# A two-layer graph network: the loads of the natural layouts and the first left operands get other places in the order of work

## The chip, the cores and the metric

The kernel runs on one core of one Trainium2 chip, in float32. The metric is the device time of one execution in microseconds (us): before the change 1774.37, the median of three runs (1773.52 to 1776.88).

## The reference, cut to what matters

`x` has 16 batches of 1024 nodes with 128 features; `adj` is a dense 1024 x 1024 matrix. Layer 0 is one graph convolution, layer 1 five steps of a gated graph unit; both are applied to a normalised, rectified input and added to `x`.

```python
# layer 0
h = relu(layernorm(x));  x = x + adj @ (h @ weight) + bias
# layer 1
h = relu(layernorm(x))
for _ in range(5):
    m  = adj @ h                          # in_matrix = out_matrix = adj
    av = concat([m, m])
    u3 = h @ u3_w.T + u3_b
    z  = sigmoid(av @ w3_w.T + w3_b + u3)
    r  = sigmoid(av @ w4_w.T + w4_b + u3)
    hv = tanh(av @ w5_w.T + w5_b + (r * h) @ u5_w.T + u5_b)
    h  = (1 - z) * h + z * hv
x = x + h
```

## The kernel before, in words

**Tiling.** Four batches form a quad, and there are four quads. A step of layer 1 for one quad is an aggregation (`adj @ h` for the four batches, `aggregate`, L439) and then its gates (`gates`, L799), which run twice: with key "A" for batches 0 and 1 and with key "B" for batches 2 and 3. Two quads are worked on in turn, a step of the one and then a step of the other (L1233), so that the state which a step has updated is needed again only a step later. In the 20 steps stand two more aggregations, for layer 0 (`BLOCKS`, L75), and two plain ones run ahead of the steps.

**The aggregation.** It is a fast matrix multiplication in two levels with seven products each, so 49 small products. One small product is two fp32 matmuls of 128 x 128 with 128 x 256 (L504), each issued as two instructions. Its left operand is a sum of blocks of `h`, its right operand a sum of blocks of `adj`. The right operands are made once at the start and kept in DRAM; 9 of them are resident in SBUF, and the other 40 are streamed in pairs (512 KB) through `ring`, which holds six pairs. `stream` (L297) loads the pair that comes six pairs later into the room of the pair that has just been used. Pair 17 is thus loaded at place 29, pair 18 at place 31, pair 19 at place 33 and pair 0 of the next aggregation at place 36. The five loads after these are put among the gates (`GATE_LOADS`, L68). Pair 18 is first used by the product of place 45.

**Left operands.** `nat[:, k]` holds the state of batch k in the natural layout, with the nodes along the partitions. The left operands are made of it: blocks of `big` by ACT copies (L401) and by sums of DVE, and blocks of `little` (L424 to L427) by sums over `big`, by DVE. The first of them for the next aggregation are made ahead, among the gates: `early_pieces` (L432) returns 12 pieces in the order

1. two ACT copies from nat[0] and nat[1],
2. four sums of `little`,
3. two more ACT copies from nat[0] and nat[1],
4. two sums of `big` from nat[2] and nat[3],
5. two more sums of `little`.

**Natural layouts.** The gates work on the transposed state. After the update, DVE transposes 32 x 32 squares (`squares_to_dram`, L664), SP stores them to a scratch in DRAM (fn<-sq), and `natural_from` (L673) loads them back as the natural layout with four DMAs of 128 KB for each batch (nat<-fn).

**What sets the order.** All is written out by hand. Every DMA is issued by SP, in program order, and a DMA that has to wait (for PE to have read a room of the ring, or for a store's data) holds up those behind it. Pieces of side work are put under a key by `put` (L708) and emitted when the program gets there by `place` (L711). Key k, 1 to 49, is after the k-th small product of the aggregation; "Ar0" to "Ar3" are after the r part of gates A for each of four halves of two batches, "Az0" to "Az3" after their z part, and the same with B. After z comes the third part (pv, tanh, hv), which has no keys.

Other side work at such keys: in some steps statistics for a later normalisation (`NORMS`, at r3, z1 and z3 of both gates, L788 to L790); in the aggregation after these the factors `nmr` (place 10), the ACT activations that use them, and the stores h<-ha or ft<-hb (places 22 and 36); in three steps transposed inputs (sqt<-ft, places 8, 18, 28 and 38); in eight steps the outputs of an earlier quad (loads at place 16, adds at 34, the store out_dram<-xt at 38).

**The lines touched.** `GATE_PLACES` (L975) has the places of the 12 early pieces, and the default of `loads_at` in `step` (L983) those of the four natural loads. `period(4)` is 30 and `period(5)` is 37. The very first step (L1231), and the loads for the aggregations of layer 0 (L1073), pass places of their own. The final step has no successor and loads nothing.

Of the kernel before, what the change touches and what calls it, by code (L numbers as in the profile page):

```python
# [96 lines left out]
def tile_two_gnn_layers(  # L97
# [30 lines left out]
    def dma(out, in_):  # L128
        pin(nc.sync.dma_start(out=out, in_=in_))
# [4 lines left out]
    def x_tile(b):  # L134
        return pre.tile([P, NC, D], F32, tag="xt", name=f"xt_{b}")

    def load_x(b, xt=None, parts=((0, NC),)):
        xt = xt if xt is not None else x_tile(b)
        for cs in parts:
            cs = slice(*cs)  # L140
            dma(xt[:, cs], by_slots(x[b])[:, cs])
        return xt
# [289 lines left out]
    def early_pieces(n):  # L432
        bigs, smalls = left_pieces(n)
        return bigs[0] + smalls[0] + bigs[1] + bigs[3] + smalls[1][:2]

    def period(i):
        return 2 + 7 * i
# [226 lines left out]
    def squares_to_dram(hT, nm):  # L664


        sq = flip_tile(f"sq_{nm}")
        for g in range(NH):
            pin(nc.vector.transpose(squares_of_half(sq, g), transposed_half(hT, g)))  # L669
        scratch, blocks = scratch_for("fn", nm)  # L670
        return lambda: dma(scratch, sq.rearrange("p k j e -> p (k j e)")), blocks
# [19 lines left out]
    def transposing(b, hT):  # L691

        box = {}

        def load():
            box["sq"] = flip_tile(f"sqt_{b}")
            dma(box["sq"].rearrange("p k j e -> p (k j e)"), parked[b][0])

        def turn():
            for g in range(NH):  # L700
                pin(nc.vector.transpose(transposed_half(hT, g), squares_of_half(box["sq"], g)))

        return load, turn
# [4 lines left out]
    def put(k, *pieces):  # L708
        fixed.setdefault(k, []).extend(pieces)
# [56 lines left out]
    def put_statistics(kind, first):  # L766

        rest = []
        for n, b in enumerate((first, first + 1)):
            box = {}  # L770

            def begin(b=b, box=box):
                box["n"] = Norm(xts[b], None, f"{kind}{b}")
                box["n"].statistics(range(CH))

            def relu(k, b=b, box=box):
                def run():
                    if k == 0:
                        box["n"].dst = flip_tile(f"h{kind}_{b}")
                    box["n"].relu(range(2 * k, 2 * k + 2))  # L780

                return run

            def done(b=b, box=box):
                (keep if kind == "a" else layer_1_input)(b, box["n"].dst)

            key = "AB"[n]
            put(f"{key}r3", begin)  # L788
            put(f"{key}z1", lambda box=box: box["n"].statistics(range(CH, NC)))
            put(f"{key}z3", lambda box=box: box["n"].scales(EVERY))  # L790
            rest.append((10, lambda box=box: box["n"].shift(EVERY)))
            rest += [(11 + 13 * n + 3 * k, relu(k)) for k in range(CH)]
            rest.append((22 + 14 * n, done))
            if kind == "a":
                rest.append((("Ar0", "Br0")[n], lambda b=b: bias(b)))
        return rest
# [175 lines left out]

    state = {}

    GATE_PLACES = ("Ar1", "Ar2", "Ar3", "Ar3", "Az0", "Az1", "Br1", "Br2", "Bz0", "Bz1", "Bz1", "Bz2")  # L975
    BLOCK_PLACES = (44, 46, 47, 47, 48, 48)

    def loads_of_next(source, places):

        for k, at in enumerate(places):  # L980
            put(at, lambda k=k: natural_from(source[k], nat[:, k]))

    def step(i, loads_at=(period(4), period(5), "Ar0", "Ar2"), early_places=GATE_PLACES):  # L983
        st = state[i]
        quad, n = st["quad"], st["step"]
        nm = f"{quad}_{n}"
        hT = [hT_all[:, i, k] for k in range(Q)]
        last = n == STEPS - 1
        final = last and quad == quads - 1
        other = state[1 - i]  # L990
        me = (quad, n)
        for k, piece in relus.pop("next", ()):
            put(k, piece)
        for b, k in LOADS.get(me, ()):
            put(k, lambda b=b: xts.update({b: load_x(b)}))
        if me in TRANSPOSED:
            q = TRANSPOSED[me]
            for k in range(Q):
                load, turn_it = transposing(q * Q + k, hT_all[:, q % 2, k])
                put(8 + 10 * k, load)  # L1000
                put(17 + 10 * k, turn_it)
        if me in OUTPUTS:
            for k, piece in zip((16, 34, 38), outputs[OUTPUTS[me]]):
                put(k, piece)
        block = BLOCKS.get(me)

        source = h0_of(block) if block else other["blocks"]
        if final:
            st["x1"] = []

            def load_x1(k):
                x1 = x_tile(f"1_{quad * Q + k}")
                dma(x1, x1s[quad * Q + k])
                st["x1"].append(x1)

            for k, places in enumerate(((None, 10, 13), (12, 24, 27), (26, 39, 41), (37, "R10", "R11"))):
                for piece, at in zip(outputs[(quad - 1) * Q + k], places):
                    if at is not None:
                        put(at, piece)
            for k, at in enumerate(("R00", "R01", "Z01", "V10")):  # L1020
                put(at, lambda k=k: load_x1(k))
        if source is not None:
            loads_of_next(source, loads_at)
        aggregate(nm, place)
        if me in NORMS:
            relus["next"] = put_statistics(*NORMS[me])
        if source is not None:
            for k, piece in zip(early_places, early_pieces(made[0])):
                put(k, piece)
        stored, ready = {}, {}  # L1030

        def turn(first):
            def run(k):
                k += first
                stored[k] = Later(lambda n: ready[k][n])

                def squares():
                    store, ready[k] = squares_to_dram(hT[k], f"{nm}_{k}")
                    if k >= Q - 2:
                        put({Q - 2: 4, Q - 1: 9}[k], store)  # L1040
                    else:
                        store()

                if k == Q - 1:
                    put(3, squares)
                else:
                    squares()

            return run

        if last:
            outputs.update({quad * Q + k: output(quad * Q + k, Later(lambda n, k=k: ready[k][n])) for k in range(Q)})
            if quad == quads - 2:
                put("Bz1", outputs[quad * Q][0])
        if final:
            last_gates(quad, hT, st["x1"])
            st["quad"], st["blocks"] = None, None
            return
        for a, key in enumerate("AB"):
            pair = slice(2 * a, 2 * a + 2)  # L1060
            gates(
                [mT[:, 2 * a + k] for k in range(2)],
                hT[pair],
                f"{nm}{key}",
                key,
                turn(2 * a),
            )
        st["step"] += 1
        st["blocks"] = [stored[k] for k in range(Q)]
        if last:  # L1070
            begin(i, quad + 2)
        if block:
            loads_of_next(other["blocks"], (period(3) + 4, period(4) + 4, period(5) + 2, period(6)))  # L1073
            pieces = early_pieces(made[0] + 1)
            for k, piece in zip(BLOCK_PLACES, pieces):
                put(k, piece)
            aggregate(f"a{block}", place, gates_follow=False)
            for k in range(Q):
                for g in range(NH):
                    po(block * Q + k, g)  # L1080
                    if 2 * k + g in (1, 2, 6, 7):
                        pieces[{1: 6, 2: 7, 6: 8, 7: 9}[2 * k + g]]()
            for piece in pieces[10:]:
                piece()
# [4 lines left out]
    def begin(i, quad):  # L1089

        if quad >= quads:
            state[i] = {"quad": None, "blocks": None}
            return
        state[i] = {"quad": quad, "step": 0, "blocks": parked_of(quad)}
# [13 lines left out]
    def h0_of(quad):  # L1108
        return Later(lambda k: h0_blocks[quad * Q + k])
# [120 lines left out]
    early_places = ("Br0", "Br1", "Br2", "Br2", "Br3", "Br3", "Br2", "Br3", "Bz0", "Bz1", "Bz2", "Bz2")  # L1230
# [45 lines left out]
```

## Time and profile before

| What | us |
|---|---|
| median of three runs | 1774.37 |
| the profiled execution's own time | 1779.16 |
| its span, first to last instruction | 1777.4 |
| PE busy (99% of the span) | 1761.9 |
| DVE busy (77%) | 1372.8 |
| ACT busy (51%) | 903.7 |
| one fp32 instruction 128 x 256 of the aggregation, mean | 0.380 |
| one ACT copy from nat (L401), median | 0.609 |
| one DVE sum of `little`, mean | 0.42 |

The granted TensorE clock is 0.999 of full speed. Matmul instructions overlap, so starts are compared rather than durations: where nothing waits, small products start every 0.863 us. DMA, all issued by SP: 396.9 MB, 223 GB/s on average; the loads of the ring are 440 of 512 KB, the natural loads nat<-fn 256 of 128 KB, with a median of 6.3 and 6.6 us from issue to landing.

How to read the rows: in the timeline a row is start, duration, engine, line, operation, output<-inputs and a count, and in brackets at its end the idle time before it with what ended it. PE is TensorE's matmul, DVE VectorE, ACT ScalarE, SPq the DMA issues of SyncE. In the table by windows each engine has busy time and instructions, then come the granted clock, the share of the DMA engines and GB/s.

### The profile page before, as it was taken

The numbers are of one execution on the slowest core, as the hardware profiler recorded it, in microseconds if no ns is written. First come the engines' busy times: TensorE is split into PE (matmuls) and PEld (weight loads), VectorE is DVE, ScalarE is ACT, GpSimd is POOL, SyncE is SP. The second block draws the span as 40 slices with busy tenths as digits, with TensorE's granted clock in tenths as the row PEclk, the third lists the DMA queues.
The fourth block names the chain that finished last, engine by engine and source line by source line (L and its number), as shares of the span: only waits on it lengthen the run. The fifth ranks groups of instructions, "written<-read, shape, count | busy, mean of one in ns | idle before, by whom it ended". The sixth has DMA issues, their size and how long they took to land.

```text
span 1777.4 us, 21433 instructions
## 1 busy us (share of the span) xinstructions
PE 1761.9 (99%) x6438; PEld 1200.4 (68%) x6438; DVE 1372.8 (77%) x2806; ACT 903.7 (51%) x1974; POOL 59.3 (3%) x41
## 2 busy tenths in 40 slices
PE   9999999999999999999999999999999999999998
PEld 3557667588586675858857667585776857667584
DVE  6778988776879687877687968777687777867787
ACT  5246556544555555554455554545445454445544
POOL 3101000000000000000000000000000000000000
PEclk9999999999999999999999999999999999999999
DMA  7489786688395856749839578694866849476794
GB/s 257 158 310 308 235 250 215 176 253 252 123 310 181 267 198 192 241 133 282 263 132 312 185 222 255 168 292 157 250 205 198 253 131 307 153 234 219 195 291 171
DMA packets 169970, 396.88 MB, mean 223 GB/s; under 512 B 18560, under 2 KB 88064, under 8 KB 169856
## 3 DMA queue, kind: packets, MB, share of 16 engines
q1 hardware_dynamic: 169856, 395.52, 70.8%
q8 instruction: 52, 0.85, 0.2%
q14 instruction: 62, 0.51, 0.1%
HBM read 314.44 MB, written 81.00 MB: 222 GB/s over the span
## 4 chain that ended last, share of the span: by engine, by line
PE 89%; DMA 5%; DVE 4%; ACT 1%; POOL 1%; issue 0%; SPq 0%; DVEq 0%; POOLq 0%
PE a L504 25%; PE c L504 12%; PE b L504 6%; PE a_a L504 3%; DMA ring<-rd 3%; PE pr_3B L808 2%; PE pr_1B L808 2%; PE pr_0B L808 2%; PE pr_2B L808 2%; PE pr_2A L808 2%; PE pr_1A L808 2%; PE pr_0A L808 2%; PE pr_3A L808 2%; PE a_a L620 2%; PE pv_0B L808 2%; PE pv_3B L808 2%
## 5 line engine op out<-in xcount | busy, mean ns | idle before, releaser
L504 PE MATMUL a<-ring,big 128*128 128x256 f32 x1120 | 288.3, 380 | 4.4 <-DMA ring<-rd 3.7
L523 ACT COPY Z<-a 128x256 f32<-128x256 f32 x480 | 177.2, 371 | 198.9 <-PE a L504 198.6
L241 DVE TENSOR_TENSOR Z<-Z,taps 128x512 f32<-128x512 f32 (+1 forms) x264 | 144.5, 554 | 167.2 <-ACT taps L523 166.9
L504 PE MATMUL c<-ring,little 128*128 128x256 f32 x960 | 246.6, 379 | 1.2 <-DMA ring<-rd 1.1
L504 PEld LDWEIGHTS a<-ring,big 128*128 128x128 f32 x1120 | 211.7, 190 | 43.5 <-issue 10.5
L241 DVE TENSOR_TENSOR mT<-mT,Z 128x1024 f32<-128x1024 f32 x154 | 188.3, 1223 | 27.4 <-ACT Z L523 22.3
L504 PEld LDWEIGHTS c<-ring,little 128*128 128x128 f32 x960 | 182.0, 190 | 26.9 <-ACT Z L523 1.5
L523 ACT COPY taps<-c 128x256 f32<-128x256 f32 x280 | 103.6, 370 | 117.2 <-PE c L504 112.5
L504 PE MATMUL b<-ring,big 128*128 128x256 f32 x560 | 143.8, 379 | 1.0 <-DMA ring<-rd 1.0
L504 PE MATMUL a<-resident,little 128*128 128x256 f32 x560 | 143.8, 379 | 0.0
L504 PE MATMUL a<-ring,little 128*128 128x256 f32 x560 | 143.7, 379 | 0.0
L504 PEld LDWEIGHTS b<-ring,big 128*128 128x128 f32 x560 | 106.3, 190 | 15.8 <-DMA ring<-rd 1.4
L504 PEld LDWEIGHTS a<-resident,little 128*128 128x128 f32 x560 | 106.3, 190 | 14.7 <-ACT Z L523 0.3
L504 PEld LDWEIGHTS a<-ring,little 128*128 128x128 f32 x560 | 106.4, 190 | 14.5
L669 DVE STREAM_TRANSPOSE sq<-hT_all 128x512 f32<-128x512 f32 x152 | 98.6, 687 | 0.0
L523 ACT COPY taps<-b 128x256 f32<-128x256 f32 x140 | 52.0, 372 | 56.7 <-PE b L504 55.8
L401 ACT COPY big<-nat 128x512 f32<-128x512 f32 x132 | 80.6, 614 | 0.1
L238 DVE TENSOR_TENSOR little<-little,big 128x256 f32<-128x256 f32 x154 | 65.4, 425 | 6.7
L238 DVE TENSOR_TENSOR little<-big 128x256 f32<-128x256 f32 x154 | 64.3, 418 | 0.0
L238 DVE TENSOR_TENSOR little<-big,little 128x256 f32<-128x256 f32 x154 | 64.2, 417 | 0.0
L241 DVE TENSOR_TENSOR little<-big 128x256 f32<-128x256 f32 x154 | 64.0, 416 | 0.2
L523 ACT COPY mT<-a 128x256 f32<-128x256 f32 x80 | 29.8, 372 | 48.1 <-PE a L504 48.0
(282 smaller groups left out, 2912.6 us busy)
## 6 DMA issues: line engine op xcount, KB each, us to landing
ring<-rd SPq DMA_DIRECT2D x440, 512.0 KB, 6.3
fn<-sq SPq DMA_DIRECT2D x76, 512.0 KB, 3.7
nat<-fn SPq DMA_DIRECT2D x256, 128.0 KB, 6.6
x1d<-xt SPq DMA_DIRECT2D x16, 512.0 KB, 5.9
sqt<-ft SPq DMA_DIRECT2D x16, 512.0 KB, 6.8
xt<-x1d SPq DMA_DIRECT2D x16, 512.0 KB, 7.6
xt<-in_x_dram SPq DMA_DIRECT2D x15, 512.0 KB, 6.2
out_dram<-xt SPq DMA_DIRECT2D x14, 512.0 KB, 7.9
```

The source lines that it names most:

```text
L238: pin(nc.vector.tensor_sub(o, a, b))
L241: pin(nc.vector.tensor_add(o, a, b))
L401: return [lambda i=i: pin(nc.scalar.copy(made_of(k, i), part(a, b, i))) for i in range(2)]
L504: nc.tensor.matmul(bank, l, right[:, c, :], start=opens and c == 0, stop=c == SB - 1, skip_group_check=True,)
L523: pin(nc.scalar.copy(to, bank))
L620: nc.tensor.matmul(bank, left[:, c, :], right[c // SB][:, c % SB], start=p in (1, 2, 5) and c == 0, stop=c == CH - 1, skip_group_check=True,)
L669: pin(nc.vector.transpose(squares_of_half(sq, g), transposed_half(hT, g)))
L808: nc.tensor.matmul(bank, w_sb[:, w, :], moving, start=start, stop=stop, skip_group_check=True)
```

## The change

Two tuples change; no instruction is added or removed. `loads_at` becomes 48, "Ar0", "Ar1", "Ar3" instead of 30, 37, "Ar0", "Ar2". In `GATE_PLACES` the first two copies go from "Ar1", "Ar2" to "Az0", "Az1", and the four sums of `little` from "Ar3", "Ar3", "Az0", "Az1" to "Az2", "Az2", "Az3", "Br0". The other six pieces stay.

```diff
@@ -972,7 +972,7 @@
-    GATE_PLACES = ("Ar1", "Ar2", "Ar3", "Ar3", "Az0", "Az1", "Br1", "Br2", "Bz0", "Bz1", "Bz1", "Bz2")
+    GATE_PLACES = ("Az0", "Az1", "Az2", "Az2", "Az3", "Br0", "Br1", "Br2", "Bz0", "Bz1", "Bz1", "Bz2")
     BLOCK_PLACES = (44, 46, 47, 47, 48, 48)
@@ -980,7 +980,7 @@
-    def step(i, loads_at=(period(4), period(5), "Ar0", "Ar2"), early_places=GATE_PLACES):
+    def step(i, loads_at=(48, "Ar0", "Ar1", "Ar3"), early_places=GATE_PLACES):
         st = state[i]
```

The pieces run by these places, unchanged:

```python
    def early_pieces(n):
        bigs, smalls = left_pieces(n)
        return bigs[0] + smalls[0] + bigs[1] + bigs[3] + smalls[1][:2]
```

## The prediction

> **What bounds the kernel now.** I read the page's busy line first, then the waits of the matmul engine, and then looked at the places of the few waits in the timeline.
>
> ```profile
> PE 1761.9 (99%) x6438; PEld 1200.4 (68%) x6438; DVE 1372.8 (77%) x2806; ACT 903.7 (51%) x1974; POOL 59.3 (3%) x41
> ```
>
> TensorE is busy for 99% of the span: it is the bound, and an edit that removes none of its instructions can only win back its idle time. The waits of PE (total us, times, longest) say whose idle time that is:
>
> ```profile
> PE a L504 <- DMA ring<-rd: 3.7, 5, 2.0
> PE c L504 <- DMA ring<-rd: 1.1, 1, 1.1
> PE b L504 <- DMA ring<-rd: 1.0, 1, 1.0
> PE a L504 <- ACT Z L523: 0.7, 3, 0.3
> ```
>
> Seven waits for a streamed right operand, three for a PSUM bank that ACT empties. To price a wait I take the distance between the starts of neighbouring products in PE's timeline and subtract 0.863 us, the distance where nothing waits (so the product after a wait, which starts 0.07 slow, is counted too). After the special start, in order of time: 0.52 (at 294, ACT), 2.20 (601, ring), 0.60 (678, ring), 0.67 (958, ring), 0.47 (1010, ACT), 1.38 (1102, ring), 0.94 and 0.29 (1114 and 1117, ring), 1.29 and 0.45 (1727 and 1729, ring): 8.81 us. The steps without a wait repeat every 76.63 us.
>
> Four of these places, 601, 678, 958 and 1114, are the same product: place 45, the first to use pair 18 of the ring. What stands ahead of that load on SP's queue, at the largest:
>
> ```profile
> 588.69 0.38 SPq L129 DMA_DIRECT2D ring<-rd  x1
> 589.17 2.26 SPq L129 DMA_DIRECT2D nat<-fn  x4
> 591.53 3.50 SPq L129 DMA_DIRECT2D ring<-rd  x3
> ...
> 600.90 5.35 SPq L129 DMA_DIRECT2D nat<-fn  x8
> ```
>
> ```profile
> 597.99 1.03 PE L504 MATMUL a<-ring,little 128*128 128x256 f32 x4
> 600.98 1.10 PE L504 MATMUL a<-ring,big 128*128 128x256 f32 x4 [1.96 <-DMA ring<-rd]
> ```
>
> The four transfers of nat[0] (place 30) are issued for 2.26 us; pair 18 (place 31) follows at 591.53, lands 9.3 us later, and PE, which could have used it at 598.85, starts at 600.98. The transfer engines are the crowded resource just there (an aggregation, its gates, and the aggregation with the stalls at 1102 and 1114):
>
> ```profile
> 1383.34:1425.69 42.35, 42.35 (x198) 37.28 (x197) 32.57 (x59) 19.55 (x51) 0.00 (x0) 1.00 0.93 290
> 1425.69:1460.00 34.31, 34.31 (x82) 15.18 (x81) 24.95 (x42) 18.20 (x28) 0.00 (x0) 1.00 0.36 118
> 1076.63:1118.98 42.35, 40.47 (x185) 34.73 (x185) 33.24 (x61) 18.13 (x48) 0.00 (x0) 1.00 1.02 309
> ```
>
> The last columns are granted clock, DMA share and GB/s: 93 to 102% of the engines in an aggregation, 36% among the gates, at full clock.
>
> **The change, part by part.** *SP's queue.* SP issues in program order, so what matters is what nat[0] passes. It goes from place 30 to 48: past pairs 18, 19 and 0 (places 31, 33, 36), and past the h/ft stores (place 36), sqt loads and out stores (place 38) where a step has them. nat[1] passes only what stands at place 38; nat[2] and nat[3] pass nothing, although their places are renamed. It happens in 18 steps; the first step, the final one and the two plain aggregations have places of their own. Per step 4 DMAs (512 KB) leave the crowded stretch, 512 KB / 290 GB/s = 1.8 us of all engines. Pair 18 can be issued as soon as the product of place 31 has ended: 2.4 us sooner in the steps at 601 and 958, 3.5 at 1114, but only 0.6 at 678, where PE itself is what it waits for; in each it also lands with 1.8 us less ahead of it. Against stalls of 2.20, 0.67, 1.23 and 0.60 that suffices: minus 4.70 us. The stalls at 1102 (pair 13, issued before nat[0]) and in the final step stay.
>
> A rule of the Trainium skill speaks against this move: "DMA: Bandwidth & Descriptors", section "Rules for kernel authors", says to overlap a transfer with compute by issuing it early and waiting late. By that rule postponing nat[0] can only lose, and the sum would be 0 or above. The row decides:
>
> ```profile
> DMA to landing us min/median/max: 2.1/6.4/11.6
> ```
>
> nat[0] and nat[1] now follow pair 0, roughly where nat[1] and nat[2] are issued today, and need that landing time. At 601 that is 600.90 to 606.25; today's last load of that group lands about 4.5 us after issue, at 611. The second copy would be due at about 613 (its place in the next paragraph, in a step without the stall). Early issue buys nothing beyond that, so I take the row; if the landing took 11.6, the rule would be right (the slower rival).
>
> *ACT.* The two copies of 0.61 us (L401) go from behind r1 and r2 to behind z0 and z1. In the step from 1425.69 the z activations run from 1433.46, 0.69 each, one per 0.86 of PE. With the copies between them: copy0 from 1434.15, z1 1434.8, copy1 1435.4, z2 1436.0, z3 to 1437.3; tanh0 starts at 1437.75 anyway. The cover is 0.45 us to tanh0. If it is gone, the queue behind copy1 is z2, z3, tanh; PE waits for the bank of z2 only at its third pv product, so another 2.5 us of lateness pass before PE stops. Cost 0.
>
> *DVE.* The four sums of little go from r3, r3, z0, z1 to z2, z2, z3 and Br0. Three end by 1437.3, before the first hv at 1438.47: 0. The fourth (0.42 us) moves into gates B. In a step with no statistics DVE idles 1.81 us there: 0. In the seven steps with statistics it is full, so it hands 0.42 us to the next aggregation, to where the normalisation's nmr is made at place 10 and ACT waits for it:
>
> ```profile
> 292.70 0.23 DVE L349 SCALAR_TENSOR_TENSOR nmr_a<-mv_a,rstd_a 128x8 f32<-128x8 f32 x2
> 292.89 0.88 ACT L362 ACTIVATE ha<-xt,nmr_a,rstd_a 128x128 f32<-128x128 f32 x2 [1.83 <-DVE nmr_a L349]
> ```
>
> Behind that activation stand the Z copies, and PE waits for their bank: a wait of 1.83 us costs 0.52, one of 1.78 costs 0.47, one of 1.11 (at 728) nothing, so a wait counts from about 1.31. With 0.42 more: plus 0.42 at 294 and plus 0.22 at 728. The four other quiet ones wait 0 to 0.7 and stay under it. At 1010 the stall should vanish, minus 0.47: DVE comes late there because it waited 6.75 us for the fourth sqt load, which is now issued some 3.9 us sooner, ahead of nat[0] and nat[1].
>
> *SP afterwards.* 12 natural loads now stand in a row ahead of pair 1, at 0.67 us each (5.35/8) about 2.7 us later than today; pair 1 is read only at the next aggregation, 35 us away: 0.
>
> The sum for the profiled execution: 1779.16 - 4.70 - 0.47 + 0.42 + 0.22 = 1774.6 (span 1777.4, and 1.8 around it). But that execution lies 4.79 us above the median 1774.37. If the difference is stalls of the same kind, as the gapless steps suggest, the median run has 8.81 - 4.79 = 4.0 us of stalls left; the net share that the change removes, 4.53 of 8.81 or 51%, is 2.1 us there. Forecast: 1774.4 - 2.1 = 1772.3.
>
> **The rivals.** *The whole stall.* The median run carries the four stalls at full size, and what it lacks of the profiled one is elsewhere: 1774.4 - 4.7 = 1769.7. For it: at 601 the delay comes from SP's order, which is the same in every run. Against it: pair 18 lands 7.3 to 9.9 us after issue in most steps and stalls nobody, so the other three are close to chance.
>
> *Hidden anyway.* Without the profiler these loads are in time, what is left is at 1102 and in the final step (1.38 + 1.74 = 3.1 of the 4.0), and the 0.6 of DVE's slip takes part of the rest: 1774.2. For it: 3 runs span 3.4 us, so stalls vary.
>
> *Slower: nat[1] lands too late for copy1.* The place is Az1; ACT stands, and PE stops at the third pv product once nat[1] lands more than 12.4 us after the gates' first matmul (9.7 for copy1, plus 0.2 for copy and pipeline, plus 2.5). At 601, issue to 606.25 plus the longest landing, 11.6, is 617.9 against 603.4 + 12.4 = 615.8: 2.1 us. Eight steps with h or ft stores have that geometry; at an average of 0.75 us, less the gain of 2.1, it gives 1774.4 + 6 - 2.1 = 1778.3. Against it: loads at that place land 3.6 to 8.4 us after issue, and the transfer engines then have 64% to spare.
>
> **How the numbers follow.** The proportional case 0.38, the whole stall 0.34, hidden 0.14, slower 0.14. A measurement of this kernel can tell about 0.2%, 3.5 us, from no change: the whole stall is then faster (0.34), the proportional case and the hidden one are within it (0.52), the late copy is slower (0.14). The range reaches from a little under the whole stall, 1769.0, to 1777.0, between hidden and slower. Within 0.2% and faster together hold most of the chance, and the likeliest case alone is 1770.8 to 1773.8.
>
> **What would show it.** Right: in the waits of PE, ring waits at place 45 are gone, the one of pair 13 and those of the final step remain; on SP the three ring loads after place 30 are issued at once after one another, with 12 natural loads behind them; the copies of L401 wait for nothing; tanh still starts 12 us after the first r matmul. Wrong: an idle time of L401 released by nat<-fn, a PE wait for a bank within the gates, more than 0.9 us at places 12 to 14 after the statistics steps, or a ring wait at place 45 with nothing natural ahead of it, which would mean that the crowding, and not nat[0], was the cause.

## The result, and the profile after

The changed kernel takes 1772.3 us (median of 22 runs, 1770.63 to 1777.01); the kernel before, over 22 runs that include the three of the prediction, 1775.88. The ratio is 0.9981, with a 95% interval of 0.9975 to 0.9987: 3.4 us less (2.3 to 4.4). That is just within the 0.2% that the prediction took as the least that can be told; the interval excludes no change.

The profiled execution took 1770.63 us, with a span of 1768.9. The waits of PE in its trace (total us, times, longest):

```profile
PE pf L927 <- DVE hT_all L241: 1.7, 2, 1.3
PE unread L149 <- DVE zeros L146: 1.5, 1, 1.5
PE pq_a L551 <- DMA big<-in_adjT_dram: 1.2, 2, 0.8
PE po L743 <- DVE xt L241: 0.8, 1, 0.8
PE pq_a L551 <- ACT nat L362: 0.5, 1, 0.5
PE a L504 <- ACT Z L523: 0.3, 1, 0.3
```

No wait for the ring is left, where there were seven. SP's queue at the step that had the largest one:

```profile
588.17 3.95 SPq L129 DMA_DIRECT2D ring<-rd  x4
592.18 1.93 SPq L129 DMA_DIRECT2D ft<-hb  x4
594.15 0.60 SPq L129 DMA_DIRECT2D x1d<-xt  x1
594.86 6.05 SPq L129 DMA_DIRECT2D nat<-fn  x8
601.18 0.35 SPq L129 DMA_DIRECT2D xt<-in_x_dram  x1
601.69 2.72 SPq L129 DMA_DIRECT2D nat<-fn  x4
```

Pairs 17, 18, 19 and 0 now go out in one run, and the natural loads follow the stores. In PE's timeline the product of place 45 follows that of place 44 at once, 0.87 us later:

```profile
597.65 1.03 PE L504 MATMUL a<-ring,little 128*128 128x256 f32 x4
598.52 1.03 PE L504 MATMUL a<-ring,big 128*128 128x256 f32 x4
```

An aggregation of the later steps and the gates behind it, in the table by windows (the last three columns are clock, DMA share, GB/s):

```profile
1376.00:1418.00 42.00, 42.00 (x195) 36.76 (x194) 32.80 (x59) 19.19 (x50) 0.00 (x0) 1.00 0.87 278
1418.00:1452.00 34.00, 34.00 (x83) 15.48 (x82) 24.26 (x40) 17.98 (x29) 0.00 (x0) 1.00 0.44 136
```

The share of the DMA engines went from 0.93 to 0.87 in the aggregation and from 0.36 to 0.44 among the gates.

The two traces can be laid over each other, stretch by stretch, by the starts of their first and last small products. The 21 stretches between aggregations differ by 0.01 us at most. The whole difference of 8.5 us between the spans lies inside eight of the 22 aggregations, those with the stalls that the prediction lists and, by 0.12 us the other way, the one at 728.

### The profile page after: what moved, and what is told of

The parts are those of the page before. It is cut to its first block, busy times and chain, and to the rows that moved or that the text cites. A ratio compares the mean times of both kernels' runs of the same rounds, so it can differ in the third digit from the quotient of the medians.

```text
span 1768.9 us, 21409 instructions
## 1 busy us (share of the span) xinstructions
PE 1759.2 (99%) x6438; PEld 1201.1 (68%) x6438; DVE 1375.1 (78%) x2806; ACT 898.1 (51%) x1974; POOL 58.8 (3%) x41
## 4 chain that ended last, share of the span: by engine, by line
PE 96%; DVE 1%; DMA 1%; POOL 1%; ACT 0%; issue 0%; SPq 0%; DVEq 0%; POOLq 0%
PE a L504 27%; PE c L504 14%; PE b L504 7%; PE a_a L504 3%; PE pr_2B L808 2%; PE pr_1B L808 2%; PE pr_0B L808 2%; PE pr_3B L808 2%; PE pr_3A L808 2%; PE pr_2A L808 2%; PE pr_0A L808 2%; PE pr_1A L808 2%; PE pr_4A L808 2%; PE pr_4B L808 2%; PE a_a L620 2%; PE pv_3A L808 2%
## 5 line engine op out<-in xcount | busy, mean ns | idle before, releaser
L401 ACT COPY big<-nat 128x512 f32<-128x512 f32 x132 | 80.7, 614 | 0.1
```

Of the source, the lines that this page charges most:

```text
L401: return [lambda i=i: pin(nc.scalar.copy(made_of(k, i), part(a, b, i))) for i in range(2)]
```

## The experiments

The theory is that the four loads of nat[0] stood on SP's queue ahead of pair 18, and that their issues and bytes together made it late. The rivals are that the later copies and sums gain, that only the bytes or only the issues count, that nat[1] and its neighbours at place 38 matter, and that it was chance. "Below before" is worked out from the ratio to the runs of the kernel before on the same chip.

### The loads alone, and the copies and sums alone

```diff
# x1_loads_only, against the kernel before
-    def step(i, loads_at=(period(4), period(5), "Ar0", "Ar2"), early_places=GATE_PLACES):
+    def step(i, loads_at=(48, "Ar0", "Ar1", "Ar3"), early_places=GATE_PLACES):
# x2_pieces_only, against the kernel before
-    GATE_PLACES = ("Ar1", "Ar2", "Ar3", "Ar3", "Az0", "Az1", "Br1", "Br2", "Bz0", "Bz1", "Bz1", "Bz2")
+    GATE_PLACES = ("Az0", "Az1", "Az2", "Az2", "Az3", "Br0", "Br1", "Br2", "Bz0", "Bz1", "Bz1", "Bz2")
```

> The kernel before with the new places of the four natural loads alone; the copies and sums stay at Ar1 to Az1. Theory (nat[0] stood in SP's queue ahead of pair 18): the whole gain of the change, about 3.5 us below before, unless the copies now wait for nat[1], which at Ar2 is due some 2 us before it lands where h or ft stores are issued; up to 2.5 us of that is hidden behind PE, so 0 to 1 us is given back. Rival (the later copies and sums are what gains): no change against before. Rival (late copies hurt): slower than before by 3 us or more.

> The kernel before with the new places of the two copies and four sums alone; the loads stay. Theory: nothing gained, 0 to 1 us slower than before by the fourth sum, which DVE hands on to place 10 after the steps with statistics. Rival (the later copies and sums are what gains): about 3.5 us below before.

Loads alone: 1773.97, ratio 0.9987 (0.9980 to 0.9994), 2.3 us below before. Copies and sums alone: 1776.19, ratio 1.0001 (0.9992 to 1.0010), no change. So the gain comes with the loads. The later copies may add something to it (0.9987 against 0.9981), but the intervals overlap. With the loads late and the copies early, the copies of L401 wait once for nat<-fn, 0.7 us in the whole span (total and times of ACT's idle time before them), and PE stops nowhere in the gates of the 18 steps for it:

```profile
  DMA nat<-fn: 0.7, 1
```

### One load less ahead, or one more

```diff
# x3_past_pair_18, against the kernel before
-    def step(i, loads_at=(period(4), period(5), "Ar0", "Ar2"), early_places=GATE_PLACES):
+    def step(i, loads_at=(32, period(5), "Ar0", "Ar2"), early_places=GATE_PLACES):
# x4_two_at_30, against the kernel before
-    def step(i, loads_at=(period(4), period(5), "Ar0", "Ar2"), early_places=GATE_PLACES):
+    def step(i, loads_at=(period(4), period(4), "Ar0", "Ar2"), early_places=GATE_PLACES):
```

> The kernel before, with nat[0] loaded at place 32 instead of 30: on SP's queue it passes pair 18 alone, and its 512 KB stay in the crowded stretch. Theory: no ring wait at place 45; most of the gain, 2.5 to 3.5 us below before, the rest lost where pair 19 is now late at place 48. Rival (what counts is the bytes taken out of the stretch, not the order): no change against before.

> The kernel before, with nat[1] loaded at place 30 too, behind nat[0]: the dose ahead of pair 18 is doubled. Theory: pair 18 is issued about 2 us later still and has 1.8 us more ahead of it; in the quiet steps it had some 2.6 us to spare, so nearly every one of the 18 steps gets a ring wait at place 45 of 1 us or more: 15 to 35 us slower than before. Rival (the stalls are chance of the crowding, whatever stands ahead of pair 18): within 4 us of before.

Moved past pair 18 alone, with its bytes still inside the aggregation, nat[0] gives 1773.96, ratio 0.9989 (0.9982 to 0.9997), 2.0 us below before (0.5 to 3.2; 2.5 to 3.5 had been expected), and no wait at place 45. SP's queue and PE in the step that had stalled longest:

```profile
588.66 0.86 SPq L129 DMA_DIRECT2D ring<-rd  x2
589.61 2.41 SPq L129 DMA_DIRECT2D nat<-fn  x4
592.12 1.31 SPq L129 DMA_DIRECT2D ring<-rd  x2
```

```profile
597.87 1.03 PE L504 MATMUL a<-ring,little 128*128 128x256 f32 x4
598.74 1.03 PE L504 MATMUL a<-ring,big 128*128 128x256 f32 x4
```

To be rid of these waits the bytes need not leave the stretch: the order is enough. With nat[1] ahead too, the time is 1786.8, ratio 1.0060 (1.0046 to 1.0075), 10.7 us above: the direction is right, the size is less than the 15 to 35 expected. PE's waits for ring operands in that run:

```profile
PE a L504 <- DMA ring<-rd: 8.2, 5, 2.3
PE b L504 <- DMA ring<-rd: 1.6, 1, 1.6
```

Four of these waits are at place 45, near 526, 605, 964 and 1119 (2.55, 2.55, 1.50 and 1.44 us, counted as in the prediction). A fifth is near 243 (0.72 us): the profile names ACT for it, but pair 18 landed 0.14 us before that product started, as in the other four. The other 13 steps, with as much ahead of pair 18, stay quiet. Why can be read in one of them, the step whose aggregation starts at 1383 in the kernel before. KB and us to landing of pair 18, first in the kernel before, then with two natural layouts ahead, and SP's row for these:

```profile
ring<-rd SPq DMA_DIRECT2D x1, 512.0 KB, 7.8
```

```profile
ring<-rd SPq DMA_DIRECT2D x1, 512.0 KB, 4.5
```

```profile
1413.73 7.22 SPq L129 DMA_DIRECT2D nat<-fn  x8
```

SP took 7.22 us to issue the eight loads. By the median of the 18 steps pair 18 was issued 5.0 us later than in the kernel before, counted from the start of the aggregation, and landed 3.8 us sooner after its issue: most of the later issue is given back by a faster landing. That the transfer engines had meanwhile worked off what was ahead would explain it, and is not shown by itself. The expectation had added 2 us of issue and 1.8 us of bytes.

### The bytes alone, and the issues alone

```diff
# y1_bytes_at_30 and y2_issues_at_30, against the changed kernel
+    idle_room = dram.tile([P, N], F32, tag="idle_room", name="idle_room")
+    def extra():
# y1: 512 KB, one DMA
+        dma(idle_room, parked_right[0].rearrange("p a c n -> p (a c n)"))
# y2: four DMAs of 2 KB
+        for k in range(4):
+            dma(idle_room[bass.ts(k, SQ), 0:16], parked_right[0][bass.ts(k, SQ), 0, 0, 0:16])
...
             loads_of_next(source, loads_at)
+            put(period(4), extra)
```

> The changed kernel with one more DMA at place 30 of the same 18 steps: 512 KB of pair 0 copied from DRAM to an unused DRAM room, one issue of some 0.4 us instead of four of 2 us. If the stall is made by the bytes ahead of pair 18 (they keep the transfer engines 1.8 us in the crowded stretch): most of the gain goes, 0 to 1 us below before. If it is made by SP's issue time ahead of pair 18: within 1 us of the changed kernel, about 3 us below before.

> The changed kernel with four more DMAs at place 30 of the same 18 steps, each of 32 rows of 64 bytes: the issues of nat[0] without its bytes. If the stall is made by SP's issue time ahead of pair 18: most of the gain goes, 0 to 1 us below before. If it is made by the bytes: within 1 us of the changed kernel, about 3 us below before.

Bytes: 1774.35, ratio 0.9986 (0.9979 to 0.9993). Issues: 1773.82, ratio 0.9985 (0.9977 to 0.9994). Each is some 2.5 us below before, about 0.8 us above the changed kernel by the ratios, and inside its interval. Neither alone takes the gain away, and neither profile has a wait at place 45 in the 18 steps. The extra transfer is a weaker dose than nat[0]: by the mean time of such packets in the trace its 512 KB, in packets of 32 KB, hold the 16 engines for 1.2 us, those of nat[0], in packets of 1 KB, for 2.1 us. By their times these two runs say only "not one of them alone"; the margins in the next section say more.

### nat[0] back in its place, twice

```diff
# y3_twice, against the changed kernel
+            put(period(4), lambda s=source: natural_from(s[0], nat[:, 0]))
             loads_of_next(source, loads_at)
# y4_nat0_back, against the changed kernel
-    def step(i, loads_at=(48, "Ar0", "Ar1", "Ar3"), early_places=GATE_PLACES):
+    def step(i, loads_at=(period(4), "Ar0", "Ar1", "Ar3"), early_places=GATE_PLACES):
```

> The changed kernel, with nat[0] loaded a second time, at place 30, where it stood before: four issues and 512 KB ahead of pair 18, and the same again at place 48. Theory (nat[0] ahead of pair 18, its issues and bytes together): the gain is gone, ring waits at place 45 are back, 0 to 2 us below before or level with it. Rival (the gain is that nat[1], and what stands at place 38, moved): within 1 us of the changed kernel.

> The changed kernel with nat[0] alone put back to place 30; nat[1] stays at Ar0, behind the stores and sqt loads of place 38, and the copies and sums stay late. Theory: level with before, at most 1 us below it, ring waits at place 45 back. Rival (nat[1] behind place 38 is what gains): the whole gain stays, about 3.3 us below before.

Loaded at place 30 and again at 48: 1775.85, ratio 0.9992 (0.9981 to 1.0003). No difference from before can be told, nor, since the intervals overlap, one from the changed kernel. But the waits at place 45 are back, in four steps (0.61, 0.40, 0.71 and 0.95 us). One of them, in PE's timeline of that run:

```profile
1110.05 1.03 PE L504 MATMUL a<-ring,little 128*128 128x256 f32 x4
1111.78 1.10 PE L504 MATMUL a<-ring,big 128*128 128x256 f32 x4 [0.71 <-DMA ring<-rd]
```

With nat[0] moved back and nat[1] left behind place 38: 1775.23, ratio 0.9990 (0.9982 to 0.9998), 1.8 us below before. The wait at place 45 is back in one step (1.97 us), but by the median half of the gain is still there: the theory had said 1 us at most. DVE's waits for the transposed input tell what nat[1] had to do with it (before, changed, nat[0] back):

```profile
DVE hT_all L701 <- DMA sqt<-ft: 20.5, 4, 6.8
```

```profile
DVE hT_all L701 <- DMA sqt<-ft: 2.4, 2, 1.9
```

```profile
DVE hT_all L701 <- DMA sqt<-ft: 8.1, 4, 3.2
```

In three steps the fourth sqt load is put at place 38. Before, it stood behind nat[0] and nat[1]; DVE waited up to 6.8 us for it at place 47, was late through both gates, made nmr late in the next aggregation, and ACT's waiting activation held the copies that empty PE's bank. With nat[0] back, it stands behind nat[0] alone: 8.1 us in all, and PE's stalls at 294 and 1010 (0.52 and 0.47 us before) stay gone, but for 0.11 us at 294 that the fourth sum costs (next experiment). The other profiles agree. In all five with nat[0] and nat[1] ahead of the fourth sqt load (before twice, x2, x3, x4) these waits of DVE are 16.1 to 20.5 us in all and PE stops near 1010; in all with nat[1] behind it they are 2.4 to 11.7 us and PE does not. So this path is worth about 0.9 us in the first profile (0.41 at 294, 0.47 at 1010); how much of the 1.8 us it is, the times do not show, since the interval reaches from 0.4 to 3.2.

### The fourth sum of DVE earlier

```diff
# x7_fourth_sum_Az3, against the changed kernel
-    GATE_PLACES = ("Az0", "Az1", "Az2", "Az2", "Az3", "Br0", "Br1", "Br2", "Bz0", "Bz1", "Bz1", "Bz2")
+    GATE_PLACES = ("Az0", "Az1", "Az2", "Az2", "Az3", "Az3", "Br1", "Br2", "Bz0", "Bz1", "Bz1", "Bz2")
```

> The changed kernel with the fourth sum of little put at Az3 instead of Br0, so that DVE hands nothing on into gates B. Theory (the slip of DVE costs 0.6 us in seven steps): 0 to 0.6 us below the changed kernel, not to be told from it; the activation at place 10 waits for nmr some 0.4 us less after the steps with statistics. Rival (the later fourth sum costs more than that): 1.5 us or more below the changed kernel.

1773.88, ratio 0.9981 (0.9974 to 0.9988): the ratio of the changed kernel. The slip itself can be seen at the activation of place 10 behind the first statistics, first in the changed kernel, then with the early sum:

```profile
292.55 0.88 ACT L362 ACTIVATE ha<-xt,nmr_a,rstd_a 128x128 f32<-128x128 f32 x2 [1.45 <-DVE nmr_a L349]
```

```profile
292.57 0.88 ACT L362 ACTIVATE ha<-xt,nmr_a,rstd_a 128x128 f32<-128x128 f32 x2 [1.12 <-DVE nmr_a L349]
```

The fourth sum makes that wait 0.33 us longer and costs PE 0.11 us there (the product after it starts late by so much in the one and not in the other).

### Each kernel once more

> The kernel before once more, for a second profile. Theory: ring waits at place 45 again, 1 to 5 us in all, not necessarily in the same steps, the one near 601 among them, since it comes from SP's order. Rival (the ring waits of the first profile were chance): they stand elsewhere or are gone.

> The changed kernel once more, for a second profile. Theory: no ring wait at place 45 in the 18 steps; ring waits in the final step and of pair 13 (near 1100) come and go, 0 to 3 us in all. Rival (the first profile was lucky): ring waits at place 45 of 1 us or more.

The kernel before: 1777.62 us, with waits at place 45 of 1.48 us at 524 and 0.74 at 1112, and 1.04 and 0.36 us at the ACT stalls near 294 and 1010. The expected one near 601 is not there, so it is chance which steps are late. (For the one at 1112 the profile names ACT; it is the product of place 45, and pair 18 landed 0.14 us before it started, as in every wait there.) The changed kernel: 1771.88 us and no wait of PE for the ring at all.

### The same idea in the final step

```diff
# z1_final_loads, against the changed kernel
-            for k, places in enumerate(((None, 10, 13), (12, 24, 27), (26, 39, 41), (37, "R10", "R11"))):
+            for k, places in enumerate(((None, 10, 13), (12, 24, 33), (33, 46, 48), (45, "R10", "R11"))):
```

> The changed kernel with the same idea used in the final step: the output loads of place 26 (ho and xt, 1 MB) go to 33 and their store and adds later, the store of place 27 to 33, the loads of place 37 to 45, so that pairs 17 to 19 have nothing ahead of them. Theory (what stands ahead of pairs 17 and 18 makes the ring waits there): the waits of the final aggregation go, 0.5 to 2.5 us below the changed kernel. Rival (the late loads make the tail wait instead): level or slower.

1771.76, ratio 0.9971 (0.9958 to 0.9984), the lowest ratio of the study. It cannot be told from the changed kernel: there are 7 runs, and the intervals overlap. Its final aggregation has no ring wait, where the runs with the bytes, the issues and the early fourth sum show 1.7 to 2.8 us there; but the two profiles of the changed kernel have none either.

## Why the prediction was right

**The bound and the place of the stalls: right.** PE's gaps were all there was to win. In the six profiles of kernels in which no whole natural layout stands ahead of pair 18 and the rest of the change is there (the changed kernel twice, bytes alone, issues alone, early fourth sum, final loads) there is no ring wait at place 45 in the 18 steps, nor in those with the loads alone and with nat[0] past pair 18. In the six profiles with nat[0] ahead there is at least one.

How close the others come can be worked out from the traces, for each of the 18 steps: the time at which PE could have started the product of place 45 (the start of place 44 plus 0.863 us), less the landing of pair 18. Below zero the pair is late.

| On SP's queue at place 30, just ahead of pair 18 | median margin, us | smallest, us | steps that wait |
|---|---|---|---|
| nat[0] and nat[1] (x4) | 0.8 | -2.3 | 5 |
| nat[0] (before, before again, x2, y3, y4) | 1.9, 2.0, 2.4, 2.2, 2.4 | -2.0 to -0.7 | 4, 2, 3, 4, 1 |
| nothing, nat[0] right behind it (x3) | 4.4 | 1.7 | 0 |
| 512 KB in one DMA (y1) | 4.7 | 1.6 | 0 |
| four DMAs of 2 KB (y2) | 5.4 | 1.9 | 0 |
| nothing (changed twice, x1, x7, z1) | 5.6 to 6.3 | 2.4 to 3.8 | 0 |

The order alone gives 2.5 us of margin, taking nat[0] out of the stretch another 1.4. Put back ahead (y3 against the changed kernel), nat[0] costs 3.6 us, the bytes of y1 cost 1.2 and the issues of y2 0.5. The prediction's sum for a quiet step, 0.6 us of earlier issue and 1.8 us of bytes, was thus of the right kind and too small: the issue is 0.6 us earlier as it said, but the landing is 3.3 us faster. What the part beyond the bytes is stays open. In both profiles of the changed kernel the pair is at least 2.4 us early in every step.

**What nat[0] passes: right, and incomplete.** Passing pair 18 is worth 2.0 us by itself (0.5 to 3.2). The prediction named the move of the sqt loads ahead of both natural loads, but counted it only at 1010 (minus 0.47). The step that failed is "plus 0.42 at 294": the same wait for the fourth sqt load, 4.26 us of it, stood behind that stall too, and it went from 0.52 to 0.11. At 728 the cost was 0.11 instead of 0.22.

**The stalls that "stay": wrong as put.** The waits of pair 13 and of the final step were absent in both profiles of the changed kernel and present in others. They vary from execution to execution. Which step is late is chance (the margin of the one at 601 was -2.0 us in one profile of the kernel before and 1.0 in the other); that the margin there is small is not.

**ACT and the landing: right.** The gates from 1418, with copies between the z activations as the prediction placed them:

```profile
1427.30 0.61 ACT L401 COPY big<-nat 128x512 f32<-128x512 f32 x1
1427.80 0.69 ACT L828 ACTIVATE z_2A<-pr_2A,bsum 128x512 f32<-128x512 f32 x1
1428.38 0.61 ACT L401 COPY big<-nat 128x512 f32<-128x512 f32 x1
1428.89 1.27 ACT L828 ACTIVATE z_2A<-pr_2A,bsum 128x512 f32<-128x512 f32 x2
1431.00 0.69 ACT L837 ACTIVATE hv_2A<-pv_2A,bsum 128x512 f32<-128x512 f32 x1 [0.84 <-PE pv_2A L808]
```

tanh0 starts 10.30 us after the first r activation, before and after. The copies wait for no load, and the natural loads land sooner after their issue, not later:

```profile
DMA to landing us min/median/max: 2.1/5.5/9.5
```

The median was 6.4. The prediction had set against this the rule of issuing early (the Trainium skill, "DMA: Bandwidth & Descriptors", "Rules for kernel authors"). Early issue had nothing to gain for these loads: later by 18 places, nat[0] is still waited for by no copy, and so the slower rival had no ground.

**The size: mechanism right, gain under-sized.** The forecast 1772.3 is the measured median, and that is luck: two misses cancel. The gain was put at 2.1 us and is 3.4, and the three runs that the forecast stood on had a median 1.5 us below that of the 22. The sum also lacked 0.9 us at 294 and 728: 0.41 us won where 0.42 was to be lost, and 0.11 lost instead of 0.22. Worked again from the first profile, after the fact: stalls removed 4.70 + 0.41 + 0.47 - 0.11 = 5.47 of 8.81, or 62%; the profiled execution stands 3.28 us above 1775.88, which leaves an estimated 5.5 us of stalls in a median run; 62% of that is 3.4. The interval, 2.3 to 4.4 us, leaves out the whole stall (4.7), hidden anyway (0.2) and slower. Taking the share of the stalls rather than all of them was the choice that held; that a median run's stalls are shared out like the profiled one's is assumed, not shown.

## What to carry to other kernels

Where one in-order queue feeds a just-in-time stream, a load with slack belongs behind the loads that have none: look at what stands ahead of the late one, and move it past that load alone first. Count every neighbour that the move reorders; here two stalls stayed gone with the moved load put back, since a second load had stayed behind its neighbours. Where waits come and go between executions, as here with the engines at 93 to 102%, a single profile tells which kind of product waits, but not how much or in which step. Then compare how early the load lands in every step, not only in those that stall: two profiles of one kernel had 4 and 2 steps waiting at place 45, but median margins of 1.9 and 2.0 us.

## What was not expected of the hardware

The landing time of pair 18, always 512 KB, ranged from 5.4 to 10.8 us over the steps of the kernel before, and was 4.5 us in a step where it was issued behind two natural layouts. Doubling what stood ahead cost 10.7 us in all, but only 1.1 us of the median margin, where issue time (2 us) and bytes (1.8 us) added up would have cost 3.8.

Loads behind pair 18 on the same queue delay it too. With nat[0] issued right after it (x3) pair 18 landed 6.6 us after its issue by the median, and 5.2 us in the changed kernel, where pairs 19 and 0 and the stores stand between; it was issued equally long after the start of the aggregation in both.
